# Moving half of the q/k projections of a batch into that batch, in an attention and feed-forward kernel on one core

## The chip, the cores and the metric

The kernel runs on one core of a Trainium2 chip. The metric is device time in microseconds. Times are given to 0.01 us; three runs of the kernel before lie between 1335.29 and 1335.87 us.

## What is computed

The input x has 4 batches of 1024 tokens with 256 features, in float32. One attention block with 16 heads of 16 features is followed by a gated feed-forward block; both have a layer norm before and after, and a residual:

```python
def attn(x, Wqkv, Wout):                      # B, S, D = 4, 1024, 256; H, Dh = 16, 16
    q, k, v = split((x @ Wqkv.T))             # each (B, H, S, Dh)
    scores = einsum("bhqd,bhkd->bhqk", q, k) / sqrt(Dh)
    e = exp(clip(scores - max(scores), -50, 50))
    a = e / (sum(e) + 1e-6)
    return concat_heads(a @ v) @ Wout.T

x = x + layernorm(attn(layernorm(x), Wqkv, Wout))
h = silu(x1 @ w1.T * s1) * (x1 @ w2.T * s2)   # x1 = layernorm(x); 256 -> 1024
h = gelu(h @ h1.T * s3); h = gelu(h @ h2.T * s4)   # 1024 -> 1024, twice
x = x + layernorm(h @ w3.T * s5)              # 1024 -> 256
```

## The kernel before

**Attention, 0 to about 658 us.** It runs batch by batch (b, four), then by group of four heads (g, four), then by half of the 512 queries (h, two). One (b, g, h) is a *unit*: 16 score tiles of 128 keys by two heads by 512 queries. For a tile TensorE makes scores (`s`, L451), ScalarE takes the exponential (`e`, L452, with no maximum subtracted), and TensorE adds `e` times the values into `acc` (L459). The score tiles have three buffers (`ps`), the exponentials a ring of eight tiles. VectorE keeps a running maximum of the exponentials (`top`, L468, in `rise`), which enters the denominator.

**The main loop (L868).** One pass, called a *turn* here, makes three score tiles, adds one or two pairs of finished tiles into `acc`, and then calls `side.take()` (L563). There are 32 units and about five and a third turns to a unit, some 170 turns in all. The work around the scores is a set of chains of `Step`s. A turn goes through the chains in order, first those in `first`, then those in `rest`, and takes from each what its `gap` allows (the number of turns since the chain's last step). **At most one step that uses TensorE is run in a turn**; steps that do not use TensorE are not limited. The PSUM tile of these steps, `misc`, has one buffer, so that a step's result must have been copied out by VectorE before the next step's matmul starts.

**What is in the chains.** `prologue(b)` makes the steps of a batch's input: layer norm statistics (`gather`, `root`), normalisation (`apply`), transposition (`transposes`, `xT`), and the projections. `project(w, m, h)` (L320) makes q (w = 0) or k (w = 1) for eight heads (m = 0 or 1, that is groups 0 and 1, or groups 2 and 3) and 512 tokens: two 128x512 matmuls (four passes in the profile, `p` L324), then two copies on VectorE: `hi` (L269) and `lo`, the rest beside `hi` (L328). `values(t)` makes v (`pv`, L315). `cq` holds q and k of one batch, with one buffer for each (w, m, hi or lo); `stack(b, g)` copies them with 32 DMAs on SP's queue into `stacks` (L413), which the scores read. It is called at the end of a unit, two groups ahead (L609 to L616), together with `slots`, a copy of v on GpSimd (L429).

**The bound.** Since no maximum is subtracted, `total` (sums of k, L349 and L350), `squares` (ScalarE, L338), `bound` (L357: four small bf16 matmuls `pn` in one `misc` tile, and a maximum on VectorE), `gauge` and `flag` (`pr`) work out per batch whether the scores can be too large. `flags` is the list of these steps.

**The end of a unit.** `unit_end` (L594) copies `acc` out (`o`, L269) and puts `divide` into the chains (`po`, L478 and L480, eight transposes in a score buffer: `side.borrowed` makes the next turn start with one tile fewer). After a batch's last group `ending` follows: transposes of the result (called `po` too, L506), the output projection `py` (L516), a layer norm and the residual, in the first turns of the next batch.

**Order of a batch's input before.** `begin(b)` (L583) puts one chain for batch b + 1: statistics, normalisation, transposes and the four projections of m = 0. When group 1 of batch b ends (g == NG - 3), v and, five turns later, the four projections of m = 1 (`qk1`) are added, and after them `flags`. So all of a batch's q and k are made during the preceding batch. Beside these run the rounding of the feed-forward weights (`check_weights`, with DMAs on GpSimd's queue, and two VectorE instructions `w` L257 for each block).

**Feed-forward, from about 658 us.** Dense matmuls (L697) that read weights from the places that q and k had; the change does not edit it.

Of the kernel before, what the change touches and what calls it, by code (L numbers as in the profile page):

```python
# [9 lines left out]
F32 = mybir.dt.float32  # L10
F32R = mybir.dt.float32r
BF16 = mybir.dt.bfloat16
I32 = mybir.dt.int32
AF = mybir.ActivationFunctionType
ALU = mybir.AluOpType
AX = mybir.AxisListType
PSUM = bass.MemoryType.PSUM

P = 128
HEADS = 16  # L20
DH = 16
SLOT = 32
HPG = P // SLOT
NG = HEADS // HPG
# [13 lines left out]
TPQ = NQ // P  # L38
# [76 lines left out]
def tile_fast(ctx: ExitStack, tc: tile.TileContext, x, wqk, wv, wo, w1, w1s, w2, w2s, h1, h1s, h2, h2s, w3, w3s, out, bad):  # L115
    nc = tc.nc
    B, S, D = x.shape
    HID = w1.shape[1]
    DC = D // P
    HC = HID // P  # L120
    NT = S // P
    NH = S // NQ
    HPT = P // DH
    GPT = HPT // HPG
# [52 lines left out]
    with ExitStack() as actx, ExitStack() as rctx:  # L177
# [90 lines left out]
        def to_vector(o, i, scale=1.0):  # L268
            nc.vector.tensor_scalar(o, i, scale, None, ALU.mult)  # L269

        def prologue(b, space, copy):

            st = {}
# [46 lines left out]
            def project(w, m, h):  # L320
                def run():
                    pp = space(f"p{w}_{b}_{m}_{h}")
                    for c in range(DC):
                        nc.tensor.matmul(pp, wqk_sb[:, c, w, HPT * m : HPT * (m + 1), :], st["xT"][:, c, h * NQ : (h + 1) * NQ], start=c == 0, stop=c == DC - 1)  # L324
                    hi, lo = (cq[w, m, k][:, h * NQ : (h + 1) * NQ] for k in ("hi", "lo"))
                    scale = 1.0 if w else 1.0 / math.sqrt(DH)
                    copy(hi, pp, scale)
                    nc.vector.scalar_tensor_tensor(lo, pp, scale, hi.bitcast(F32), ALU.mult, ALU.subtract)  # L328

                return run  # L330

            kinds = [(w, m) for w in range(2) for m in range(DC)]

            def squares(w, m, h):
                def run():
                    sq = st["sq", w, m] = work.tile([P, NQ], BF16, tag="sq", name="sq", bufs=4)
                    hi = cq[w, m, "hi"][:, h * NQ : (h + 1) * NQ].bitcast(F32)
                    nc.scalar.activation(sq, hi, AF.Square)  # L338

                return run  # L340

            def total(m):
                def run():
                    if m == 0:
                        st["norm"] = work.tile([P, NT], F32, tag="norm", name=f"norm_{b}", bufs=1)
                        st["sum"] = work.tile([P, DC], F32, tag="sum", name="sum", bufs=1)
                        st["sum2"] = work.tile([P, DC], BF16, tag="sum2", name="sum2", bufs=1)
                    t = st["sum"][:, m : m + 1]
                    nc.vector.tensor_reduce(t, cq[1, m, "hi"].bitcast(F32), AX.X, ALU.add)  # L349
                    nc.gpsimd.tensor_tensor(st["sum2"][:, m : m + 1], t, t, ALU.mult)  # L350

                return run

            def bound(h):


                def run():  # L357
                    pn = space(f"pn_{b}_{h}")
                    for k, (w, m) in enumerate(kinds):
                        nc.tensor.matmul(pn[SLOT * k : SLOT * (k + 1), :], heads_bf, st["sq", w, m], start=True, stop=True)  # L360
                    nc.vector.tensor_reduce(st["norm"][:, TPQ * h : TPQ * (h + 1)], pn.rearrange("p (t n) -> p t n", n=P), AX.X, ALU.max)

                return run

# [7 lines left out]
            def flag():  # L372

                pr = space(f"pr_{b}")
                for i in range(2):
                    nc.tensor.matmul(pr[0:1, i * P : (i + 1) * P], st["kinds"][:, i : i + 1], ident, start=True, stop=True)
                for m in range(DC):
                    nc.tensor.matmul(pr[0:1, 2 * P + SLOT * m : 2 * P + SLOT * (m + 1)], st["sum2"][:, m : m + 1], heads_bf, start=True, stop=True)

                qs, ks = (pr[0:1, 0 : 2 * P].rearrange("p (i w n) -> p i w n", i=2, w=2)[:, :, w, :] for w in range(2))  # L380
                top = work.tile([1, P // 2], F32, tag="ktop", name="ktop", bufs=1)
                nc.vector.tensor_reduce(top, ks.rearrange("p i n -> p n i"), AX.X, ALU.max)

                nc.vector.scalar_tensor_tensor(top, top, S * S / SPREAD, pr[0:1, 2 * P : 2 * P + P // 2], ALU.mult, ALU.add)
                bounds = work.tile([1, 2, P // 2], F32, tag="bounds", name="bounds", bufs=1)
                nc.vector.tensor_mul(bounds, qs, top.unsqueeze(1).to_broadcast([1, 2, P // 2]))
                most = work.tile([1, 2], F32, tag="most", name="most", bufs=1)
                nc.vector.tensor_reduce(most, bounds, AX.X, ALU.max)
                k = counts + 2 * b

                for i, limit in enumerate((SAFE, math.log(S / FULL))):
                    limit = 0.98 * limit * limit * S * S / (1 + SPREAD)
                    nc.vector.tensor_scalar(misses[0:1, k + i : k + i + 1], most[:, i : i + 1], limit, 0.0, ALU.is_le, ALU.is_equal)
# [2 lines left out]
            xt = [[Step(apply(h, i), 1, False) for i in range(0, TPQ, 2)] + [Step(transposes(h, c), 1) for c in range(DC)] for h in range(NH)]  # L396
            qk = [[[Step(project(w, m, h), 1) for w in (1, 0)] for h in range(NH)] for m in range(DC)]
            v = [Step(values(t), 1) for t in range(0, NT, 2)]
            flags = [Step(total(m), 1, False) for m in range(DC)]
            for h in range(NH):  # L400
                flags += [Step(squares(w, m, h), 1, False) for w, m in kinds] + [Step(bound(h), 1)]
            return norm, xt, qk, v, flags + [Step(gauge, 0, False), Step(flag, 1)]

        def copies(g, w, c0=0, c1=S):

# [19 lines left out]
        def slots(b, g, t0=0, t1=NT):  # L425


            def run():
                nc.gpsimd.tensor_copy(  # L429
                    vaug[g % 2][:, t0:t1, :, 0:DH], cv[:, t0:t1, HPG * DH * g : HPG * DH * (g + 1)].rearrange("p t (h e) -> p t h e", e=DH)  # L430
                )
                slotted[g % 2] = b, g, t1

            return run
# [116 lines left out]
        class Side:  # L551
# [4 lines left out]
                self.borrowed = False  # L556

            def add(self, steps, first=False):
                chain = [list(steps), self.slot]
                (self.first if first else self.rest).append(chain)  # L560
                return chain

            def take(self):  # L563
# [16 lines left out]
        side = Side()  # L580
        accs, tops, ends, later = {}, {}, {}, {}

        def begin(b):  # L583

            if b + 1 < B:
                norm, xt, qk, v, flags = prologue(b + 1, misc, to_vector)

                qk1 = sum(qk[1], [])
                qk1[0].gap = 3
                later["rest"] = v, qk1 + [Step(lambda: side.add(flags), 0, False)]  # L590

                later["chain"] = side.add([Step(lambda: None, 0 if b else 4, False)] + sum((norm[h] + xt[h] for h in range(NH)), []) + sum(qk[0], []))

        def unit_end(b, g, h):  # L594

            o = both.tile([P, NQ], F32, tag="o", name="o", bufs=2)
            to_vector(o, accs[b, g, h])

            assert g or not b or not any(step.tensor for step in ends[b - 1, h][0])
            unit = side.add(divide(g, h, o, tops[b, g, h]), True)  # L600
            if g == NG - 1:
                unit[0].extend(ending(b, h, to_scalar if (b, h) == (B - 1, NH - 1) else to_vector))
                ends[b, h] = unit
            if h < NH - 1:
                return

            n, at = g + 2, b
            if n >= NG:
                n, at = n - NG, b + 1  # L609
            if b == B - 1 and g == NG - 2:  # L610
                load_weights("h1", range(HC // 2))
            if at < B:
                if at > b:
                    assert not later["chain"][0]
                stack(at, n)
                slots(at, n)()  # L616
            if g == NG - 3 and b + 1 < B:
                v, qk1 = later["rest"]
                assert not later["chain"][0]
                later["chain"][0].extend(v)  # L620
                side.add([Step(lambda: None, 5, False)] + qk1)
            elif g == NG - 3:
                side.add([Step(lambda n=n: load_weights(n), 1, False) for n in ("w1", "w2", "w3")])
                side.add([Step(lambda: None, 7, False)] + prepare(0, to_vector))
            if g == NG - 1:
                begin(b + 1)


# [196 lines left out]
        def first_copy(*args):  # L825
            (to_scalar if alone else to_vector)(*args)

        norm, xt, qk, v, flags = prologue(0, first_space, first_copy)

        queues = [nc.scalar] + [nc.gpsimd, nc.sync] * 3 + [nc.gpsimd]  # L830

# [20 lines left out]
        stack(0, 1)  # L852
        load_rest()
        early = [v[1], Step(slots(0, 0, 0, NT // 2), 0, False)]
        side.add(early + v[2:] + [Step(slots(0, 0), 0, False), Step(slots(0, 1), 0, False)] + sum(qk[1], []) + [Step(lambda: side.add(flags), 0, False)])
        begin(0)
        side.add([s for k in blocks for s in check_weights(*k)])
        made = seen = weighed = 0

# [270 lines left out]
```

## Time and profile before

| | us |
|---|---|
| median of three runs | 1335.56 (1335.29 to 1335.87) |
| the profiled execution, its own time | 1335.65 |
| its span in the profile | 1333.7 |
| busy in the span: PE, PEld, DVE, ACT, POOL | 1271.8, 797.1, 724.3, 696.6, 120.7 |
| from the first unit's end to the last unit's end | 57.63 to 658.44 |
| batch 1, 2, 3 from unit end to unit end | 161.43, 157.59, 140.58 |

PE is TensorE's matmuls, PEld its weight loads, DVE VectorE, ACT ScalarE, POOL GpSimd. The span is what the trace covers; the execution's own time is 1.95 us longer. A line such as L324 is a line of the kernel before. In a row of the timeline the first number is the start, the second the length.

### The profile page before, as it was taken

How to read it: one execution, taken by the hardware profiler on the slowest of the kernel's cores; microseconds unless marked ns; L12 is line 12 of the kernel's file. 1: busy time of each engine (PE TensorE's matmuls, PEld its weight loads, DVE VectorE, ACT ScalarE, POOL GpSimd, SP SyncE). 2: the span in 40 equal slices, each digit the busy share in tenths (PEclk: the TensorE clock that was granted, in tenths of full speed). 3: DMA queues.
4: the chain of work that ended last, by engine and by line, in shares of the span. 5: the costliest groups of instructions: out<-in, count | busy, mean ns of one | idle time of the engine just before them, and what ended most of it. 6: DMA issues, size and time to landing. Idle time of an engine off the chain costs nothing.

```text
span 1333.7 us, 18779 instructions
## 1 busy us (share of the span) xinstructions
PE 1271.8 (95%) x7042; PEld 797.1 (60%) x7042; DVE 724.3 (54%) x1561; ACT 696.6 (52%) x847; POOL 120.7 (9%) x166
## 2 busy tenths in 40 slices
PE   7999999999999999989999999999999999999996
PEld 3334333343343434333478888888888888888885
DVE  3575669756696455645482553735436364362623
ACT  4587788877887787888741321414224141231410
POOL 6120112111111000000000000000000000000000
PEclk9999999999999999999999999999999999999998
DMA  4675344544444433235220000000000000000000
GB/s 133 152 194 111 98 97 113 122 111 99 120 106 106 77 64 62 45 64 179 79 111 1 1 16 1 17 0 0 16 1 16 0 16 2 0 17 0 17 0 19
DMA packets 38661, 79.61 MB, mean 60 GB/s; under 512 B 11296, under 2 KB 21152, under 8 KB 38560
## 3 DMA queue, kind: packets, MB, share of 16 engines
q1 hardware_dynamic: 30672, 53.66, 18.3%
q0 software_dynamic: 7360, 24.12, 5.5%
q8 instruction: 58, 0.95, 0.3%
q10 hardware_dynamic: 528, 0.52, 0.1%
q14 instruction: 43, 0.35, 0.1%
HBM read 28.98 MB, written 15.73 MB: 34 GB/s over the span
## 4 chain that ended last, share of the span: by engine, by line
PE 78%; DVE 9%; ACT 7%; issue 2%; POOL 1%; DMA 0%; SPq 0%; ACTq 0%; POOLq 0%; DVEq 0%
PE ph L697 35%; PE acc L459 13%; PE s L451 8%; ACT e L452 6%; PE pg L697 6%; PE pz L750 4%; PE p L324 4%; PE py L516 2%; PE pv L315 2%; DVE top L468 2%; PE po L480 1%; DVE o L269 1%; DVE sg L713 1%; DVE st L93 1%; DVE ha_lo L702 1%
## 5 line engine op out<-in xcount | busy, mean ns | idle before, releaser
L452 ACT ACTIVATE e<-s 128x1024 f32<-128x1024 f32 x512 | 486.3, 1036 | 131.1 <-PE s L451 117.8
L459 PE MATMUL acc<-e,vaug 128*32 128x512 f32 x2048 | 256.5, 603 | 2.9 <-POOL vaug L429 2.9
L733 ACT ACTIVATE a<-ph,h_scale 128x512 f32<-128x512 f32 x128 | 81.0, 685 | 306.9 <-PE ph L697 306.9
L451 PE MATMUL s<-sq,sk 64*128 64x512 f32 x1024 | 193.9, 449 | 24.7 <-ACT e L452 22.7
L697 PE MATMUL ph<-hb_lo,h 128*128 128x512 f32 x512 | 199.4, 389 | 0.0
L697 PE MATMUL ph<-hb_hi,h 128*128 128x512 f32 x512 | 199.4, 389 | 0.0
L451 PEld LDWEIGHTS s<-sq,sk 64*128 64x128 f32 x1024 | 86.3, 184 | 159.4 <-ACT e L452 124.5
L468 DVE TENSOR_TENSOR top<-top,e 128x512 f32<-128x512 f32 x192 | 134.1, 699 | 35.7 <-ACT e L452 30.1
L459 PEld LDWEIGHTS acc<-e,vaug 128*32 128x32 f32 x2048 | 49.4, 109 | 108.5 <-issue 98.1
L734 DVE CAST ha_hi<-a 128x512 fp32r<-128x512 f32 x64 | 27.1, 424 | 158.2 <-ACT a L733 158.2
L103 POOL TENSOR_TENSOR rstd<-ve,minus_half 128x4 f32<-128x4 f32 (+1 forms) x33 | 37.5, 1136 | 791.6 <-DVE ve L101 791.6
L697 PEld LDWEIGHTS ph<-hb_lo,h 128*128 128x128 f32 x512 | 96.1, 188 | 20.1
L697 PEld LDWEIGHTS ph<-hb_hi,h 128*128 128x128 f32 x512 | 96.1, 188 | 20.2
L697 PE MATMUL ph<-ha_hi,sq 128*128 128x512 f32 x256 | 101.9, 398 | 0.4
L697 PE MATMUL ph<-ha_lo,sq 128*128 128x512 f32 x256 | 99.8, 390 | 0.0
L697 PE MATMUL ph<-ha_lo,sk 128*128 128x512 f32 x256 | 99.7, 390 | 0.0
L697 PE MATMUL ph<-ha_hi,sk 128*128 128x512 f32 x256 | 99.7, 390 | 0.0
L713 DVE SCALAR_TENSOR_TENSOR sg<-pg,w_scale,sg 128x512 f32<-128x512 f32 x64 | 47.1, 745 | 47.7 <-ACT sg L711 47.7
L711 ACT ACTIVATE sg<-pg,w_scale 128x512 f32<-128x512 f32 x64 | 43.3, 688 | 56.6 <-DVE ha_lo L702 48.4
L734 DVE CAST hb_hi<-a 128x512 fp32r<-128x512 f32 x64 | 27.0, 422 | 82.2 <-ACT a L733 82.2
L324 PE MATMUL p<-xT,wqk_sb 128*128 128x512 f32 x128 | 64.0, 626 | 0.9 <-ACT xT L266 0.9
L697 PEld LDWEIGHTS ph<-ha_hi,sq 128*128 128x128 f32 x256 | 48.2, 188 | 12.7 <-DVE sg L713 3.4
(145 smaller groups left out, 1663.6 us busy)
## 6 DMA issues: line engine op xcount, KB each, us to landing
w<-in_h_dram POOLq DMA_DIRECT2D x16, 512.0 KB, 4.6
h_r<-wr POOLq DMA_DIRECT2D x16, 512.0 KB, 3.8
sk<-ck1hi SPq DMA_DIRECT2D x64, 64.0 KB, 2.3
sk<-ck1lo SPq DMA_DIRECT2D x64, 64.0 KB, 2.3
sq<-cq1hi SPq DMA_DIRECT2D x64, 64.0 KB, 2.3
sq<-cq1lo SPq DMA_DIRECT2D x64, 64.0 KB, 2.3
h<-h_r SPq DMA_DIRECT2D x8, 512.0 KB, 6.5
sk<-ck0hi SPq DMA_DIRECT2D x56, 64.0 KB, 2.3
```

The source lines that it names most:

```text
L103: nc.gpsimd.tensor_tensor(rstd[:, :n], ve[:, :n], self.minus_half[:, :n], ALU.pow)
L324: nc.tensor.matmul(pp, wqk_sb[:, c, w, HPT * m : HPT * (m + 1), :], st["xT"][:, c, h * NQ : (h + 1) * NQ], start=c == 0, stop=c == DC - 1)
L451: nc.tensor.matmul(s[:, a, :], stacks[1, g % 2, u][r, c * P : (c + 1) * P], stacks[0, g % 2, u][r, h * NQ : (h + 1) * NQ], start=True, sto ...
L452: nc.scalar.activation(pair(k)[:, u], s, AF.Exp)
L459: nc.tensor.matmul(acc[SLOT * i : SLOT * (i + 1), :], vaug[g % 2][:, c, i, :], pair(k)[:, i // 2, i % 2, :], start=c == 0, stop=c == NT - 1)
L468: nc.vector.tensor_max(top, top if c > 1 else pair(k - 2)[:, :, :, 0:P], pair(k)[:, :, :, 0:P])
L697: nc.tensor.matmul(p, homes[n][c][:, m * P : (m + 1) * P], half[:, c, :], start=c == 0 and k == 0, stop=c == len(homes[n]) - 1 and k == 1)
L711: nc.scalar.activation(sg, p[:, 0, :], AF.Silu, scale=scales["w1"][:, m : m + 1])
L713: nc.vector.scalar_tensor_tensor(sg, p[:, 1, :], scales["w2"][:, m : m + 1], sg, ALU.mult, ALU.mult)
L733: nc.scalar.activation(a, p[:, j, :], AF.Gelu, scale=scales[n][:, m : m + 1])
L734: nc.vector.tensor_copy(o[0][:, m, :], a)
L750: nc.tensor.matmul(p[t], half[:, c, t * P : (t + 1) * P], homes["w3"][c], start=c == 0 and k == 0, stop=c == HC - 1 and k == 1)
```

## The change

It has four parts.

1. The projections of m = 1 (q and k of heads 8 to 15) are no longer made in the preceding batch. `begin(b)` puts those of batch b itself at the head of all chains (`first=None`, a new case of `Side.add`), with a gap of two turns from batch 1 on. For batch 0, where they had been early already, v and these projections form that leading chain.
2. `begin(b)` starts only the statistics of batch b + 1, both halves together. Its transposes, projections of m = 0 and the bound of m = 0 are added by `go_on`, when the leading chain is through.
3. v is a chain of its own, begun at the same place as before (the end of group 1). `slots` of the next batch is put behind v if v is not through.
4. The bound is split by m: `bound(m, h)` uses two of the four small matmuls and a maximum over 64 partitions; there are four for a batch instead of two. `norm`, `sum` and `sum2` have two buffers. The layout of the flag's reductions follows (its last product is made in two instructions).

The diff, cut to its core:

```diff
@@ prologue
-            def bound(h):
+            def bound(m, h):
                 def run():
-                    pn = space(f"pn_{b}_{h}")
-                    for k, (w, m) in enumerate(kinds):
-                        nc.tensor.matmul(pn[SLOT * k : SLOT * (k + 1), :], heads_bf, st["sq", w, m], start=True, stop=True)
-                    nc.vector.tensor_reduce(st["norm"][:, TPQ * h : TPQ * (h + 1)], pn.rearrange("p (t n) -> p t n", n=P), AX.X, ALU.max)
+                    pn = space(f"pn_{b}_{m}_{h}")
+                    for w in range(2):
+                        nc.tensor.matmul(pn[SLOT * (2 * m + w) : SLOT * (2 * m + w + 1), :], heads_bf, st["sq", w, m], start=True, stop=True)
+                    own = slice(2 * SLOT * m, 2 * SLOT * (m + 1))
+                    nc.vector.tensor_reduce(st["norm"][own, TPQ * h : TPQ * (h + 1)], pn[own, :].rearrange("p (t n) -> p t n", n=P), AX.X, ALU.max)
...
-            flags = [Step(total(m), 1, False) for m in range(DC)]
-            for h in range(NH):
-                flags += [Step(squares(w, m, h), 1, False) for w, m in kinds] + [Step(bound(h), 1)]
-            return norm, xt, qk, v, flags + [Step(gauge, 0, False), Step(flag, 1)]
+            flags = []
+            for m in range(DC):
+                flags.append([Step(total(m), 1, False)])
+                for h in range(NH):
+                    flags[m] += [Step(squares(w, m, h), 1, False) for w in range(2)] + [Step(bound(m, h), 1)]
+            flags[-1] += [Step(gauge, 0, False), Step(flag, 1)]
+            return norm, xt, qk, v, flags
@@ begin
-        def begin(b):
-
-            if b + 1 < B:
-                norm, xt, qk, v, flags = prologue(b + 1, misc, to_vector)
-
-                qk1 = sum(qk[1], [])
-                qk1[0].gap = 3
-                later["rest"] = v, qk1 + [Step(lambda: side.add(flags), 0, False)]
-
-                later["chain"] = side.add([Step(lambda: None, 0 if b else 4, False)] + sum((norm[h] + xt[h] for h in range(NH)), []) + sum(qk[0], []))
+        def begin(b, lead=()):
+
+            _, _, qk, _, flags = own.pop(b)
+            if b + 1 < B:
+                own[b + 1] = prologue(b + 1, misc, to_vector)
+                norm, xt, qk_next, v, flags_next = own[b + 1]
+
+                later["chain"] = side.add([Step(lambda: None, 0 if b else 4, False)] + sum(norm, []))
+                later["v"] = v
+
+            def go_on():
+                side.add(flags[0] + flags[1] if b == 0 else flags[1])
+                if b + 1 < B:
+
+                    later["chain"][0].extend(sum(xt, []) + sum(qk_next[0], []) + flags_next[0])
+
+            left = sum(qk[1], [])
+            for step in left:
+                step.gap = 2 if b else 1
+            later["left"] = side.add(list(lead) + left + [Step(go_on, 0, False)], None)
@@ unit_end
                 stack(at, n)
-                slots(at, n)()
+                if at > b and later["v"]:
+                    assert n == 0
+                    later["v"].append(Step(slots(at, n), 0, False))
+                else:
+                    slots(at, n)()
             if g == NG - 3 and b + 1 < B:
-                v, qk1 = later["rest"]
-                assert not later["chain"][0]
-                later["chain"][0].extend(v)
-                side.add([Step(lambda: None, 5, False)] + qk1)
+                v = later["v"]
+                later["v"] = side.add(v)[0]
...
-            if g == NG - 1:
+            if g == NG - 1 and b + 1 < B:
                 begin(b + 1)
```

## The prediction

> **What bounds the kernel now.** I read the page's busy times first, then the same by stage (the windows view cut at the `o` copies that end each batch), then the TensorE timeline in a crowded and in an empty stretch, last VectorE's timeline at a batch's start.
>
> ```profile
> PE 1271.8 (95%) x7042; PEld 797.1 (60%) x7042; DVE 724.3 (54%) x1561; ACT 696.6 (52%) x847; POOL 120.7 (9%) x166
> L452 ACT ACTIVATE e<-s 128x1024 f32<-128x1024 f32 x512 | 486.3, 1036 | 131.1 <-PE s L451 117.8
> ```
>
> PE at 95% hides two regimes, which the stages show (columns: stretch, its length, busy PE, PEld, DVE, ACT, POOL, clock, DMA):
>
> ```profile
> 57.63:198.84 141.21, 135.00 (x849) 53.50 (x850) 89.59 (x181) 109.49 (x122) 22.73 (x32) 0.99 0.52 127
> 198.84:360.27 161.43, 152.74 (x981) 61.61 (x981) 111.24 (x245) 126.34 (x138) 29.59 (x37) 1.00 0.46 110
> 360.27:517.86 157.59, 149.93 (x967) 60.91 (x968) 102.24 (x219) 123.68 (x136) 18.80 (x24) 1.00 0.40 86
> 517.86:658.44 140.58, 128.38 (x889) 48.24 (x889) 78.28 (x168) 121.28 (x131) 5.25 (x6) 1.00 0.37 85
> ```
>
> The last batch, which prepares no other, is 17 to 21 us shorter than batches 1 and 2, and TensorE idles 12.2 us in it. So the side work costs time where it stands. A turn with a projection, from batch 1 (three score tiles, one or two pairs into `acc`, the projection):
>
> ```profile
> 260.93 0.96 PE L451 MATMUL s<-sq,sk 64*128 64x512 f32 x6
> 261.82 1.06 PE L459 MATMUL acc<-e,vaug 128*32 128x512 f32 x8
> 262.82 1.98 PE L324 MATMUL p<-xT,wqk_sb 128*128 128x512 f32 x4
> 264.73 0.97 PE L451 MATMUL s<-sq,sk 64*128 64x512 f32 x6
> 265.63 1.92 PE L459 MATMUL acc<-e,vaug 128*32 128x512 f32 x16
> 267.49 1.98 PE L324 MATMUL p<-xT,wqk_sb 128*128 128x512 f32 x4
> ```
>
> Nothing stands in brackets: TensorE never waits. The first turn takes 264.73 - 260.93 = 3.80 us, the second to 269.40, 4.67 us. Two turns with no side step, in batch 3:
>
> ```profile
> 599.71 0.96 PE L451 MATMUL s<-sq,sk 64*128 64x512 f32 x6
> 600.61 1.06 PE L459 MATMUL acc<-e,vaug 128*32 128x512 f32 x8
> 601.60 0.51 PE L451 MATMUL s<-sq,sk 64*128 64x512 f32 x2
> 602.30 0.49 PE L451 MATMUL s<-sq,sk 64*128 64x512 f32 x2 [0.20 <-ACT e L452]
> 603.22 0.50 PE L451 MATMUL s<-sq,sk 64*128 64x512 f32 x2 [0.42 <-ACT e L452]
> 603.64 1.92 PE L459 MATMUL acc<-e,vaug 128*32 128x512 f32 x16
> 605.50 0.96 PE L451 MATMUL s<-sq,sk 64*128 64x512 f32 x6
> ```
>
> They take 1.89 and 3.90 us, and TensorE waits for exponentials between. At a batch's start a third resource is full: after 198.84 no row of VectorE's timeline up to 213.90 has an idle time before it, for example
>
> ```profile
> 206.29 0.66 DVE L468 TENSOR_TENSOR top<-top,e 128x512 f32<-128x512 f32 x1
> 206.87 0.73 DVE L111 TENSOR_SCALAR y<-y,mv,rstd 128x256 f32<-128x256 f32 x2
> 207.52 0.68 DVE L269 TENSOR_SCALAR oT<-po 128x512 f32<-128x512 f32 x1
> ```
>
> [...] PE is over 90% busy in all four batches, with and without waits. [...] four `pn` take 0.40 us together, one 384 ns; so two will cost nearly what four do. [...]
>
> **The change part by part.** In both programs' instruction order TensorE has the same scores, `acc`, projections, v and transposes; only `pn` comes in 16 groups of two instead of 8 of four. I counted the turns by their side step: 51 with a dear one (`p`, `pv`, `py`) in both, 31 with a divide and 28 with a light one (`pt`, `po` L506, `fpt`) in both, with `pn` or `pr` 12 before and 20 after, empty 43 before and 35 after.
>
> *Projections.* Units between `o` copies: 415.96 to 437.33 has four projections, 21.37 us; the three from 573.25 to 623.95 have none and are 16.90 on average. So one costs (21.37 - 16.90) / 4 = 1.12 us (1.91 of TensorE, less waits that it fills). Batch 0 loses four (-4.5), batch 3 gains four (+4.5), batches 1 and 2 lose and gain four: 0. The new place in batch 3 decides. It isn't among its empty turns: the projections alternate with `po` L506 and `py` in the batch's first seven turns, and the divide of unit 0 waits behind them. These turns are TensorE's already, so I take the full price. Its bounds: 1.5 at most (a projection in a turn with two `acc` pairs against the 3.1 us of three exponentials), 0.3 at least (two turns, one with a projection and one without, are 6.5 us of TensorE against 6.2 of three-tile exponentials twice). No DMA moves: the 32 DMAs on SP stay at the unit's end, some four turns after the last projection, where they had been ready far longer; cost 0, and a few us of their lateness are covered by a whole group before the copies are read. GpSimd's four more products lie beside everything; its v copies keep their unit ends, since v ends a turn before.
>
> *The bound.* Eight empty turns become `pn` turns: a turn with `pn` or `pr` takes 3.00 us on average, an empty one 2.78, so 8 x 0.22 = +1.8 us. Bounds: 0 and 3.5 (their eight maxima, 8 x 0.69 = 5.5 us of VectorE, two thirds exposed, as VectorE is about two thirds busy).
>
> *Less crowding.* Dear turns straight after a dear one fall from 34 to 25. Means of turns by own and preceding kind, times the new counts, give +1.0 in place of +1.8: -0.8.
>
> *Squares.* ScalarE's squares outside turns with a dear step fall from 25 to 17. Six turns of one shape took 20.51 us with four squares (319.04 to 339.55) and 19.79 without (605.50 to 625.29): 0.18 each, so -1.4; bounds 0 and 8 x 0.6 = -4.8.
>
> *VectorE at the batch's start.* In batch 1's first unit (198.84 to 218.12, 19.28 us) VectorE idles 0.77 us: 18.5 us of work. After come two projections' copies (4 x 0.62 from start to start), four more statistics with their ends (4 x 0.55) and a root (0.17); two `y` copies (1.24) and four normalisations (1.3) leave: +2.3, 20.8 us, 1.5 more than the unit. The copies of a projection free the only `misc` tile, so what is late on VectorE delays the next side step of TensorE, with scores and `acc` queued behind it. Batch 2 (360.27 to 379.74, idle 0.72): 18.7 + 2.3 = 21.0 against 19.47, 1.5 too. In batch 3 VectorE has no such load, 0. Of these 3.0 us I take two thirds, +2.0, as the next unit has less to do; bounds 0 (all dissolves there) and 4 (the copies also wait for their projections, with the rest queued behind them).
>
> *Divides.* The delayed divide of unit 0 comes to stand in the turn before unit 1's in batch 2, two turns before in batches 1 and 3. Each takes one of three score buffers, and leaves ScalarE short: a divide turn is 3.37 us after a dear turn, about 4.5 after an empty one. I take 1.2 for the neighbours and 0.3 for each of the others, +1.8; bounds 0 and 3.
>
> Sum: 0 + 1.8 - 0.8 - 1.4 + 2.0 + 1.8 = +3.4 us. The profiled execution took 1335.65 us (span 1333.7 and 1.95 around it), 0.09 above the median; 1335.65 + 3.4 = 1339.05, 1339.0 beside the median.
>
> **The rivals.** A measurement of this kernel can tell about 0.2%, 2.7 us, from no change: below 1332.9 is faster, above 1338.2 slower.
> - *Spreading pays* (faster). Batch 3's 12.2 us of idle TensorE take up its four projections at 0.3 each: +1.2 - 4.5 + 1.8 - 0.8 - 1.4 = -3.7, 1332.0. It decides once a projection there costs under half its price in batch 0. For it: the waits in the empty turns. Against it: the new places are beside `py`, where no wait stands.
> - *Zero sum* (same). VectorE's lag dissolves and the divides don't collide: 0 + 1.8 - 0.8 = +1.0, 1336.6. For it: equal counts of dear turns.
> - *VectorE becomes the bound* at the starts of batches 1 and 2 (slower by more): 4 for its lag, 3 for the divides, 1.8 for `pn`: +8.8, 1344.4. For it: the timeline without gaps; against it: after one unit the load falls to 13 us a unit.
> - That the projections don't move isn't open: the order shows them in the batch's first turns.
>
> **How the numbers follow.** My sum 0.46, spreading 0.16, zero sum 0.22, VectorE 0.16. The sum's own spread puts some 0.38 of its 0.46 above 1338.2 and the rest within. Slower 0.38 + 0.16 = 0.54; faster 0.15; same 0.31. Range: 1332.5 (just above spreading's full gain) to 1344.5 (VectorE's case).
>
> **What would show it.** Batch 0 from unit end to unit end about 4 to 5 us shorter than its 141.21, batch 3 about 5 us longer than its 140.58, batches 1 and 2 longer by 1 to 3 us each; after a batch's start TensorE's side steps wait for VectorE, and `s` waits for `e` around the paired divides; feed-forward unchanged at 675 us. Wrong would be batch 3 growing by under 2 us, or batches 1 and 2 shrinking.

## The result and the profile after

The changed kernel takes **1338.55 us** (median of 11 runs, 1337.74 to 1341.84). The kernel before, run beside it, takes 1335.56 us (median of 11 runs, 1334.27 to 1338.57). The ratio is 1.0022, with a 95% interval of 1.0013 to 1.0031: slower by 3.0 us. The prediction was 1339.0 us, 1332.5 to 1344.5, slower at 0.54.

The profiled execution of the changed kernel took 1339.87 us (span 1338.1), 4.2 us more than the profiled one before, so the trace holds about one microsecond more than the medians do. Of the code lines shown here, those from 324 on have moved down by 2 to 6: `p` is now L326, the divide's transposes `po` L484 and L486, the running maximum `top` L474.

The page's busy times of the changed kernel, and its costliest group:

```profile
PE 1274.8 (95%) x7042; PEld 798.9 (60%) x7042; DVE 731.7 (55%) x1573; ACT 697.9 (52%) x847; POOL 118.8 (9%) x166
L458 ACT ACTIVATE e<-s 128x1024 f32<-128x1024 f32 x512 | 486.5, 1033 | 134.4 <-PE s L457 119.5
```

As many matmuls as before; TensorE is busy 3.0 us longer, VectorE 7.4 us. The averages say no more than that. The same four stages as before, cut at the `o` copies that end each batch (stretch, its length, busy PE, PEld, DVE, ACT, POOL, clock, DMA):

```profile
57.70:190.21 132.51, 125.64 (x833) 50.34 (x834) 86.71 (x178) 109.45 (x122) 21.41 (x31) 1.00 0.56 135
190.21:354.54 164.33, 153.39 (x977) 62.21 (x977) 112.78 (x247) 126.67 (x138) 28.21 (x37) 0.99 0.46 108
354.54:516.10 161.56, 151.90 (x971) 61.88 (x972) 104.53 (x223) 124.40 (x136) 18.60 (x24) 0.99 0.38 83
516.10:662.88 146.78, 136.14 (x901) 50.92 (x901) 84.78 (x179) 121.41 (x131) 6.17 (x7) 0.99 0.37 82
```

Batch 0 is 8.7 us shorter than its 141.21, batches 1, 2 and 3 are 2.9, 4.0 and 6.2 us longer. After 662.88 come 675.2 us of feed-forward, against 675.3 before. So 13.1 us are lost in three batches and 8.7 us are won in the first; 4.4 us are left between these two executions, and 3.0 us between the medians.

**Batch 3** has the four projections in its first seven turns. TensorE's timeline of the changed kernel there, then in a later turn of the batch, without a side step:

```profile
524.78 0.96 PE L457 MATMUL s<-sq,sk 64*128 64x512 f32 x6
525.67 1.06 PE L465 MATMUL acc<-e,vaug 128*32 128x512 f32 x8
527.60 1.98 PE L326 MATMUL p<-xT,wqk_sb 128*128 128x512 f32 x4 [0.86 <-DVE oT L269]
529.51 0.73 PE L457 MATMUL s<-sq,sk 64*128 64x512 f32 x4
...
585.52 0.50 PE L457 MATMUL s<-sq,sk 64*128 64x512 f32 x2 [0.34 <-ACT e L458]
586.44 0.50 PE L457 MATMUL s<-sq,sk 64*128 64x512 f32 x2 [0.41 <-ACT e L458]
587.35 0.50 PE L457 MATMUL s<-sq,sk 64*128 64x512 f32 x2 [0.41 <-ACT e L458]
587.79 3.22 PE L465 MATMUL acc<-e,vaug 128*32 128x512 f32 x16
```

In the first, the bracket says that the projection stood 0.86 us until VectorE had copied the `oT` that precedes it out of `misc`; that turn takes 529.51 - 524.78 = 4.73 us and not 3.80. In the second, 16 matmuls take 3.22 us and not 1.92: TensorE's granted clock was halved from 588.3 us on, for 3.41 us. That turn takes 5.41 us, and 4.12 in the kernel before. Such a stretch does not come in every execution: in the traces of experiments 1, 2 and 6, which have the four projections and no halved clock in batch 3, the batch takes 145.2 us, 4.6 more than before and not 6.2.

**Batch 0** holds, beside the 4.5 us of the forecast, a gain that nothing in the prediction foresaw. TensorE's timeline at the first divide, before:

```profile
57.86 0.63 PE L478 MATMUL po<-ident,top 128*128 128x128 f32 x4 [2.20 <-DVE top L468]
58.37 0.66 PE L480 MATMUL po<-ident,o 128*128 128x128 f32 x4
58.95 0.94 PE L451 MATMUL s<-sq,sk 64*128 64x512 f32 x4
59.83 3.33 PE L459 MATMUL acc<-e,vaug 128*32 128x512 f32 x16
```

and after, where a projection (55.66) stands ahead of the divide:

```profile
58.46 1.92 PE L465 MATMUL acc<-e,vaug 128*32 128x512 f32 x16
60.32 0.66 PE L484 MATMUL po<-ident,top 128*128 128x128 f32 x4
60.81 0.60 PE L486 MATMUL po<-ident,o 128*128 128x128 f32 x4
```

Before, the divide waited 2.20 us for VectorE's running maximum, and then 16 matmuls took 3.33 us in place of 1.92: TensorE's clock was halved, from 59.3 us for 3.41 us. After, neither. The two turns took 5.26 + 6.48 us before and 3.80 + 3.77 us after, 4.2 us less for the same steps.

**Batches 1 and 2** give up and take on four projections each, and are together 6.9 us longer. The worst turn is that of the divide of batch 2's unit 1. TensorE's timeline there, before:

```profile
394.76 1.92 PE L459 MATMUL acc<-e,vaug 128*32 128x512 f32 x16
396.62 0.66 PE L478 MATMUL po<-ident,top 128*128 128x128 f32 x4
```

after:

```profile
394.49 1.92 PE L465 MATMUL acc<-e,vaug 128*32 128x512 f32 x16
396.34 0.50 PE L457 MATMUL s<-sq,sk 64*128 64x512 f32 x2
399.51 0.66 PE L484 MATMUL po<-ident,top 128*128 128x128 f32 x4 [2.67 <-DVE top L474]
400.11 0.75 PE L486 MATMUL po<-ident,o 128*128 128x128 f32 x4
400.79 1.22 PE L457 MATMUL s<-sq,sk 64*128 64x512 f32 x4
401.94 1.93 PE L465 MATMUL acc<-e,vaug 128*32 128x512 f32 x8
```

and VectorE's after, over the same time:

```profile
396.40 0.42 DVE L494 TENSOR_TENSOR on<-po,den 128x256 f32<-128x256 f32 x1
396.75 0.68 DVE L257 SCALAR_TENSOR_TENSOR w<-w,wr 128x512 f32<-128x512 f32 x1
397.35 0.08 DVE L257 DVE_READ_ACCUMULATOR w<-w,wr 128x1 f32 x1
397.35 2.10 DVE L474 TENSOR_TENSOR top<-top,e 128x512 f32<-128x512 f32 x2
399.38 0.68 DVE L269 TENSOR_SCALAR o<-acc 128x512 f32<-128x512 f32 x1
```

The divide's first transposes need the unit's last running maximum. VectorE has no idle time here: the maximum stands behind the previous divide's arithmetic, a layer norm and a weights' block, and is done only at 399.45. TensorE works in order, so scores and `acc` wait behind the transposes for 2.67 us; then eight matmuls take 1.93 us instead of 1.06, the clock halved again, from 400.5 us for 3.41 us. The turn took 7.50 us against 4.79 before with the same steps; the next, with a transposition step more, 4.08 against 2.02 (1.68, if its last score tile is counted with the turn after it).

How much of this is the halved clock, the kernel of experiment 8 shows. Up to batch 3 it has the same steps as the changed kernel and the same waits, but no halved clock in batches 1 and 2:

```profile
400.16 0.66 PE L484 MATMUL po<-ident,top 128*128 128x128 f32 x4 [2.67 <-DVE top L474]
400.76 0.65 PE L486 MATMUL po<-ident,o 128*128 128x128 f32 x4
401.35 0.73 PE L457 MATMUL s<-sq,sk 64*128 64x512 f32 x4
402.01 1.06 PE L465 MATMUL acc<-e,vaug 128*32 128x512 f32 x8
```

The wait is again 2.67 us, but the eight matmuls take 1.06. Its batches 1 and 2 take 162.90 and 160.20 us, 1.5 and 2.6 more than in the kernel before. So of the 6.9 us, 4.1 come from the steps and their waits, and 2.8 from the two halved stretches.

### The profile page after: what moved, and what is told of

Its sections match the earlier page's. It is cut to its first block, busy times and chain, and to the rows that moved or that the text cites. A ratio compares the mean times of both kernels' runs of the same rounds, so it can differ in the third digit from the quotient of the medians.

```text
span 1338.1 us, 18787 instructions
## 1 busy us (share of the span) xinstructions
PE 1274.8 (95%) x7042; PEld 798.9 (60%) x7042; DVE 731.7 (55%) x1573; ACT 697.9 (52%) x847; POOL 118.8 (9%) x166
## 4 chain that ended last, share of the span: by engine, by line
PE 75%; DVE 12%; ACT 7%; issue 3%; SPq 1%; DMA 1%; ACTq 0%; POOL 0%; POOLq 0%; DVEq 0%
PE ph L721 35%; PE acc L465 13%; PE s L457 8%; ACT e L458 6%; PE pz L774 4%; PE pg L721 4%; PE p L326 4%; PE py L522 2%; DVE top L474 2%; PE pv L317 2%; DVE sg L737 1%; PE po L486 1%; DVE st L93 1%; DVE o L269 1%; DVE ha_lo L726 1%
## 5 line engine op out<-in xcount | busy, mean ns | idle before, releaser
L474 DVE TENSOR_TENSOR top<-top,e 128x512 f32<-128x512 f32 x192 | 136.2, 710 | 34.8 <-ACT e L458 29.0
L326 PE MATMUL p<-xT,wqk_sb 128*128 128x512 f32 x128 | 63.9, 625 | 4.2 <-DVE oT L269 3.1
```

Of the source, the lines that this page charges most:

```text
L474: nc.vector.tensor_max(top, top if c > 1 else pair(k - 2)[:, :, :, 0:P], pair(k)[:, :, :, 0:P])
```

## The experiments

"Turn 95" is the turn of 7.50 us, counted from 0 (the very first pass, which has nothing to add into `acc` yet, is left out); batches 1, 2 and 3 begin at turns 43, 86 and 128. Each kernel was timed beside the kernel before, whose medians were 1335.57, 1335.70 and 1337.16 us in the three sittings; ratios are to the runs beside, and not always the quotient of two such medians. What is said against the changed kernel by medians is against its 1338.55 us, from yet another sitting. "At one clock" compares runs whose mean granted TensorE clock was the same; the table after experiment 9 has them.

**1. The bound of m = 0 left out of batches 1 to 3.**

```diff
+                        nc.vector.memset(st["norm"], 0.0)
-                    ... + [Step(bound(m, h), 1)]
+                    ... + ([Step(bound(m, h), 1)] if m or not b else [])
```

> The changed kernel without the bound's matmuls and maxima for m = 0 in batches 1 to 3: six turns with two pn become empty turns (the squares and sums stay; norm is set to 0, so this part of the bound is left out). The prediction's price of a pn turn is 0.22 us: 6 x 0.22 = 1.3 us less than the changed kernel's 1338.55, about 1337.2. Rival one: pn lies beside waits anyway, 0 to 0.5 us less. Rival two: pn also makes TensorE wait for the squares on ScalarE and holds the one misc tile until VectorE is done, 3 us less or more.

Measured: 1339.89 us (1337.96 to 1341.56), ratio 1.0026 (1.0014 to 1.0037). By medians not faster than the changed kernel, at one clock 0.3 us faster (five runs against two), where 1.3 was forecast. The trace shows `pv` steps moving into the turns that lost their `pn`. So the added `pn` turns cost little, if anything, and the loss is elsewhere.

**2. and 3. The delayed divide put at the head of the chains**, in batch 2 alone (the first line added) and in every batch (the second), so that it follows its unit at once and no two divides are neighbours:

```diff
-            unit = side.add(divide(g, h, o, tops[b, g, h]), True)
+            unit = side.add(divide(g, h, o, tops[b, g, h]), None if (b, g, h) == (2, 0, 0) else True)
+            unit = side.add(divide(g, h, o, tops[b, g, h]), None if (g, h) == (0, 0) else True)
```

> The changed kernel, with the divide of batch 2's first unit put at the head of all chains, so that it comes right after its unit and not in the turn before the next unit's divide. Theory of the paired divides: turns 95 and 96 of the changed kernel took 7.50 and 4.08 us against 4.79 and 1.68 before, and at the same place now there is one divide alone: 3 to 5 us less than 1338.55, about 1334.5. Rival (VectorE's lag): the divide only meets VectorE's backlog there, and wherever it is moved the backlog is paid: at most 1 us less. Rival (price as predicted): 1.2 us less, 1337.3.

> The same for the first unit of every batch; in batches 1 and 3 the two divides stood two turns apart. Theory of the paired divides: batches 1 and 3 give about 0.5 to 1 us each beyond the run with batch 2 alone, 1333 to 1334. Rival (prediction's price): 1.8 us less than 1338.55 in all, 1336.8. Rival (VectorE's lag): at most 1 us less in all.

Measured: 1342.05 us (1339.46 to 1345.78), ratio 1.0049 (1.0033 to 1.0066), and 1346.93 us (1345.58 to 1348.85), ratio 1.0087 (1.0070 to 1.0104): 3.5 and 8.4 us slower than the changed kernel, at one clock 2.5 and 6.6. No expectation had them slower. TensorE's timeline of the first of them at the divide that was moved:

```profile
372.58 1.06 PE L465 MATMUL acc<-e,vaug 128*32 128x512 f32 x8
377.38 1.09 PE L484 MATMUL po<-ident,top 128*128 128x128 f32 x4 [3.74 <-DVE top L474]
378.26 1.06 PE L486 MATMUL po<-ident,o 128*128 128x128 f32 x4
379.25 1.22 PE L457 MATMUL s<-sq,sk 64*128 64x512 f32 x4
380.40 3.32 PE L465 MATMUL acc<-e,vaug 128*32 128x512 f32 x16
```

Straight after its unit the divide waits 3.74 us, with no second divide near it, and turn 95 is still 6.63 us long with its neighbour gone. The theory of paired divides falls: a divide waits for the running maximum wherever it comes soon after its unit while VectorE is behind.

**4. The next batch's statistics behind the four projections** (batches 1 and 2):

```diff
-                later["chain"] = side.add([...] + sum(norm, []))
+                later["chain"] = side.add([...] + ([] if b else sum(norm, [])))
-                    later["chain"][0].extend(sum(xt, []) + ...)
+                    later["chain"][0].extend((sum(norm, []) if b else []) + sum(xt, []) + ...)
```

> The changed kernel, with the statistics of the next batch's input (in batches 1 and 2) taken only when the batch's own four projections are through, so that VectorE has about 5 us less to do in the crowded turns. Theory of VectorE's lag: turns 45, 46, 48, 88, 90 and 91 of the changed kernel are 0.7 to 1.2 us each above what TensorE alone needs in them, about 5 us; the prediction counted 2.0. So 2 to 4 us less than 1338.55, 1334.5 to 1336.5. Rival: the lag is made up by the copies that wait for their projections, not by the statistics, and the paired divides stay: within 0.7 us of 1338.55.

Measured: 1340.29 us (1338.88 to 1341.84), ratio 1.0035 (1.0023 to 1.0048), 1.7 us slower than the changed kernel by medians, and no different at one clock (one run against two). The batch's first turns do get shorter (turns 45, 46 and 48 by 0.6, 0.8 and 0.8 us). But the statistics now stand ahead of the maximum that the next divides need. VectorE's and TensorE's timelines of this kernel in batch 1:

```profile
234.66 0.42 DVE L93 BATCH_NORM_STATS2 st<-x 128x6 f32<-128x256 f32 x1
...
235.86 1.00 DVE L101 TENSOR_SCALAR ve<-mv 128x4 f32<-128x4 f32 x1
236.77 0.68 DVE L474 TENSOR_TENSOR top<-top,e 128x512 f32<-128x512 f32 x1
```

```profile
237.59 1.08 PE L484 MATMUL po<-ident,top 128*128 128x128 f32 x4 [4.00 <-DVE top L474]
```

The divide in turn 53 waits 4.00 us, and the turn takes 8.53 us instead of 4.30; turn 95 takes 9.55. Batches 1 and 2 come out at 164.59 and 161.48 us, against 164.33 and 161.56. Moved within VectorE's queue, the work took the loss with it.

**5. A later divide.** After units of group 0 the divide comes two turns later than otherwise (a gap of three in place of one):

```diff
-            return [Step(run, 1)]
+            return [Step(run, 3 if g == 0 else 1)]
```

> The changed kernel, with the divides of group 0 (both halves, all batches) run two turns after their unit's end at the earliest. New theory (the divide waits for VectorE): a divide's first transposes need the unit's last running maximum, which stands behind VectorE's backlog in the first two units of a batch; the run with the divide right after the unit (7.55 and 7.57 us for that turn) lost 2.5 us more at each place. Two turns later the maximum should be there: turn 95's 7.50 falls to about 3.4 to 4.3 and the halved TensorE clock that followed goes, turn 53 gains about 1: 3 to 6 us under the changed kernel's 1338.55, 1333 to 1335.5. Rival (the backlog is a fixed amount of VectorE work, paid by the next side step wherever the divide stands): within 1 us of 1338.55. Rival (paired divides, score buffers): the divides are still three turns apart, 2 to 4 us less, without a change of the wait for the maximum.

Measured: 1337.84 us (1335.4 to 1342.18, 22 runs), ratio 1.0016 (1.0008 to 1.0023), 0.7 us less than the changed kernel (0.7 to 1.2 at one clock), about as the rival of the fixed backlog had it. Turn 95 falls from 7.50 to 4.06 us; turns 96 and 99 give back 1.7 and 2.4. The side steps that now come first need VectorE as well.

**6. Less work for VectorE: the rounding of the weights pauses in the first 14 turns of batches 1 to 3.** Nothing is left out; its two VectorE instructions for each block, its casts on GpSimd and its DMAs, come later.

```diff
                 for chain in self.first + self.rest:
+                    if chain is later.get("weights") and self.slot < later.get("hold", 0):
+                        continue
...
         def begin(b, lead=()):
+            later["hold"] = side.slot + 14 if b else 0
...
-        side.add([s for k in blocks for s in check_weights(*k)])
+        later["weights"] = side.add([s for k in blocks for s in check_weights(*k)])
```

> The changed kernel, with the chain that rounds the feed-forward weights paused in the first 14 turns of batches 1 to 3; about four VectorE instructions of 0.7 us in each of the first two units go elsewhere, to places with empty turns. Theory (the divide and the side steps wait for VectorE's backlog): 2.4 us less VectorE work in batch 1's and in batch 2's first two units, so 2 to 4 us under 1338.55, 1334.5 to 1336.5, with shorter turns 45 to 48, 88 to 91 and 95. Rival (the backlog is made by copies that wait for their projections): within 0.7 us of 1338.55.

Measured: **1334.22 us** (1330.97 to 1335.24, 22 runs), ratio 0.9981 (0.9975 to 0.9988): 4.3 us less than the changed kernel. TensorE's timeline at turn 95:

```profile
397.28 0.66 PE L484 MATMUL po<-ident,top 128*128 128x128 f32 x4 [1.05 <-DVE top L474]
```

1.05 us in place of 2.67, no halved clock behind it, and 5.80 us for the turn. Turns 45 and 46 fall from 5.82 and 3.28 to 5.23 and 2.64, turns 90 and 96 from 5.02 and 4.08 to 4.42 and 2.70. This is the experiment that carries the theory: with the change's own steps all in place, pausing other work of VectorE takes the loss away. At turn 95 the wait is 1.62 us shorter. VectorE's timelines there show 1.2 us of it as two weights' blocks (0.61 us each, from start to start) that are gone from ahead of the maximum, and 0.4 as the unit's last two maxima, which take 1.70 us in place of 2.10 beside GpSimd's copy `vaug`. The pause also takes work off GpSimd and its DMA queue, and no run takes it off VectorE alone.

**7. The same pause in the kernel before.**

> The kernel before, with the same hold as in e5_hold (the rounding of the feed-forward weights pauses in the first 14 turns of batches 1 to 3); nothing else is changed. In the changed kernel the hold brought 1338.55 to 1334.22, 4.3 us. Theory (the crowd on VectorE at the starts of batches 1 and 2 is the change's doing: its copies of projections came on top of the statistics and the weights' rounding): the kernel before has no such crowd, so the hold brings it little, 0 to 1.5 us, 1334.2 to 1335.7, about where the changed kernel with the hold stands; the divides of units 0 and 1 in batch 2 keep their turns of about 5 us. Rival (the weights' rounding costs that much at any batch's start, with the change or without it): 4 us here too, 1331.5, and the changed kernel stays 3 us behind the kernel before whatever is held.

Measured: 1335.64 us (1334.58 to 1337.88, 14 runs), ratio 0.9998 (0.9990 to 1.0006): no gain against 1335.70, and 1.5 us against the median of its own sitting, 1337.16. At one clock the pause brings the kernel before 2.1 to 2.3 us (0.6 at 0.994, a single run), and the changed kernel 3.9 to 4.2. In the traces, without the 1.6 us of one halved stretch in each kernel with the pause, batches 1 and 2 get 1.7 us shorter in the kernel before and 4.6 in the changed one (against the trace of experiment 8). So about half of what the pause removes, or more, is a crowd that the change made; theory and rival were both right in part. The rival's other half fails: with the pause in both, the changed kernel is not 3 us behind but 0.7 to 0.8 us ahead at 0.992 and 0.993.

**8. and 9. The price of the four projections in each place.** In the changed kernel those of batch 3 are left out, in the kernel before those that batch 0 makes for batch 1:

```diff
-            left = sum(qk[1], [])
+            left = sum(qk[1], []) if b < B - 1 else []
```

```diff
-                qk1 = sum(qk[1], [])
+                qk1 = sum(qk[1], []) if b else [Step(lambda: None, 0, False)]
```

> The changed kernel without the four m = 1 projections of batch 3 (left out, the scores there read the q and k of batch 2): their price in the new place. The prediction: 4.5 us (4 x 1.12), so 1334.0; the trace's batch 3 grew by 6.2 us, of which a halved clock window is about 1.3, so up to 5: 1333.5. Rival (spreading pays): 1.2 us, 1337.3.

> The kernel before without the four m = 1 projections that batch 0 makes for batch 1 (left out, the scores of batch 1 read batch 0's q and k): their price in the old place. The prediction: 4.5 us, 1331.1. Rival (batch 0's 8.6 us shorter trace after the change is all projections): 8 us, 1327.5. If it is about 4.5, the other 4 us of batch 0's gain come from the first unit's divide, which waited 1.9 us longer before and was followed by a halved clock.

Measured: 1332.38 us (1329.37 to 1335.06, 18 runs), ratio 0.9971 (0.9963 to 0.9979), and 1332.66 us (1329.85 to 1335.49, 22 runs), ratio 0.9975 (0.9967 to 0.9984). In the new place the four cost 1338.55 - 1332.38 = 6.2 us, in the old one 1335.70 - 1332.66 = 3.0. Both prices need a correction, since TensorE's clock differed between the runs. The mean spans (us) of the runs with three of the mean granted clocks, the number of runs in brackets:

| kernel | 0.992 | 0.993 | 0.994 |
|---|---|---|---|
| before | 1336.0 (21) | 1335.3 (26) | 1333.4 (41) |
| changed | 1337.1 (2) | 1336.4 (5) | none |
| 1: no bound of m = 0 | 1336.8 (5) | none | none |
| 2: divide first, batch 2 | 1339.6 (2) | none | 1337.7 (1) |
| 3: divide first | 1343.7 (1) | none | none |
| 4: statistics later | 1337.1 (1) | none | none |
| 5: later divide | 1336.4 (9) | 1335.2 (2) | 1335.1 (7) |
| 6: pause | 1332.9 (4) | 1332.5 (3) | 1330.6 (8) |
| 7: pause, before | 1333.7 (2) | 1333.2 (5) | 1332.8 (1) |
| 8: none in batch 3 | 1331.2 (2) | 1330.8 (12) | none |
| 9: before, none in batch 0 | none | 1330.6 (7) | 1329.6 (2) |
| 10: pause and later divide | none | none | 1329.5 (2) |

At one clock the new place costs 5.6 to 5.9 us and the old one 3.8 to 4.7; the turns that held them in the old place (29 to 37) shrink by 4.2 in the trace. Without the four, batch 3 takes 139.60 us, 5.6 less than with them and no halved clock, but also 1.0 less than in the kernel before: there the other side steps fall on other turns. So the move from batch 0 to batch 3 is dearer by up to 3 us, and its exact size stays open. The table also splits the result: at one clock the changed kernel is 1.1 us behind, and the rest of its 3.0 us goes with a median clock of 0.992 against 0.994. The clock need not be a cause from outside, though. In the changed kernel's profiled execution three halved stretches lie inside the attention after its start, from 284.5, 400.5 and 588.3 us, where the kernel before has one, at 59.3.

**10. Pause and later divide together**, in the changed kernel:

> The changed kernel with both the hold of e5_hold and the late divide of e9_late_divide (after units of group 0 a divide comes three turns after its unit and not one). Theory (a divide only shows VectorE's backlog, and the hold has removed most of the backlog): turn 95 falls from e5_hold's 5.80 to about 4, a neighbour gives part of it back, and the time is that of e5_hold within 1 us, 1333.5 to 1335. Rival (the divide's wait and the backlog are two costs that add): 4.3 + 0.7 us and the 1.8 of turn 95, 1332.0 to 1333.

Measured: **1330.28 us** (1329.16 to 1333.83, 6 runs), ratio 0.9961 (0.9946 to 0.9976). It beats both kernels, and is 8.3 us below the changed one, where the two edits alone gave 4.3 and 0.7. Both expectations were too high, the theory's by more. At a clock of 0.994 both together are at 1329.5 us of span (2 runs) and the pause alone at 1330.6 (8 runs): there the later divide brings 1.1 us, about what it brings without the pause, and the two edits about add, as the rival said. The rest of the 8.3 us goes with the clock. TensorE's waits for the running maximum and for the flag's `kinds` from 195 to 480 us (us in total, times, longest), for the kernel before, the changed one, the pause and both:

```profile
PE po L478 <- DVE top L468: 1.9, 5, 0.8
```

```profile
PE po L484 <- DVE top L474: 4.3, 4, 2.7
PE pr L378 <- DVE kinds L372: 2.1, 1, 2.1
```

```profile
PE po L484 <- DVE top L474: 2.6, 4, 1.1
PE pr L378 <- DVE kinds L372: 2.1, 1, 2.1
```

```profile
PE po L484 <- DVE top L474: 0.6, 2, 0.3
```

In batch 1 both together are 3.2 us shorter in the trace than the pause alone (159.26 against 162.49): in the new order of steps the flag's `pr` no longer waits 2.1 us, and no halved clock follows. In batch 2 they are 1.6 us longer (159.16 against 157.60): turn 95 falls from 5.80 to 4.07, but turns 96 and 99 take 0.9 and 1.7 us more. So even with the backlog removed a part is handed to the next side steps, as in experiment 5. The wait of `pr` is followed by a halved clock at 284.5 us in the changed kernel and at 286.3 us in the kernel with the pause. With both edits the profiled execution has no halved clock between 15.3 and 1319.2 us, and three of the six runs had a mean clock of 0.996, where 106 runs of the kernel before reach 0.995 at most. Its batch 3 is 4.2 us longer than that of the kernel before, close to the predicted price of four projections, and batches 1 and 2 together 0.6 us shorter.

## Why the prediction was right, and where only by cancelling

The time, the sign and the feed-forward were right, and so was the outline: batch 0 shorter, batch 3 longer, a loss at the starts of batches 1 and 2. That +3.4 came so near to the measured 3.0 us is luck in part, since only 1.1 of the 3.0 are left at one clock, and the sum had no term for the clock. Step by step:

- **Projections, 4.5 us in each place.** Right for the old place (3.0 by medians, 3.8 to 4.7 at one clock, 4.2 in the trace). For the new place the two readings differ: leaving the four out saves 5.6 to 6.2 us, 1.4 to 1.55 us each and not 1.12, but batch 3 grew by only 4.6 us where no halved clock lies in it. The other 1.6 of its 6.2 us are that clock. "In batch 3 VectorE has no such load, 0" was wrong: the timeline shows a projection there waiting 0.86 us for VectorE's copy of `oT`, in every trace with these projections, so that this wait is within the 4.6.
- **The bound, +1.8.** Its parts came as forecast (two `pn` take 0.39 us where four took 0.40; the maximum over 64 partitions takes 677 to 695 ns, that over 128 took 657 to 692); the price in time is not shown. Experiment 1 took six of the eight added groups away and gained nothing by medians, and 0.3 us at one clock. The averages of turns "with `pn`" and "empty" came from turns that differ in more than the `pn`; an added step moves the others.
- **Less crowding -0.8, squares -1.4.** Not tried by themselves; open.
- **VectorE at the batch's start, +2.0, and the divides, +1.8.** The mechanism of the first was right. Together they were to cost 3.8, 0.3 of it in batch 3. Batches 1 and 2 grew by 4.1 where their clock was not halved (the trace of experiment 8), which is near, and by 6.9 with two halved stretches; the pause takes all of the 4.1 away. The reason given for the second was wrong. Score buffers and ScalarE do not make the divide dear; it waits for the running maximum behind VectorE's backlog (2.67 us in turn 95), and pairing adds little: in experiment 2, without its neighbour, turn 95 still takes 6.63 of the 7.50 us (the neighbour's arithmetic is itself a part of the backlog). So `s` does not wait for `e` around the divides, as was expected: there, ScalarE waits for `s` (3.26 us in turn 95). The prediction counted what VectorE had to do and divided it by the unit's length; it did not ask which of VectorE's instructions TensorE stands in front of.
- **Batch 0, -4.5.** It became 8.7 shorter. The missing 4.2 us are the first divide's wait of 2.20 us and the halved clock, both in the trace of before at 57.9 to 63 us. That turn was not looked at, since the batch as a whole seemed to lose only projections.

The sum was to be -4.5 in batch 0 and about +8 in the others; it was -8.7 and +13.1 in the trace. Without the three halved stretches the +13.1 would be 8.7 (1.5, 2.6 and 4.6), close to the forecast. So two things that the prediction did not price had opposite signs and nearly cancelled: 4.2 us won at the first divide of batch 0, and 4.4 us lost to halved clocks later. Of the rivals, "VectorE becomes the bound" named the place of the loss in batches 1 and 2, with a size (1344.4) that is too high. The 1336.6 of "zero sum" lies below the interval of the ratio (1337.3 to 1339.7 us), but its +1.0 is what is left at one clock; its reasons fail, since VectorE's lag did not dissolve. "Spreading pays" had put 1.2 us for the four projections in batch 3, and is refuted by the 4.6 of the traces and the 5.6 to 6.2 of experiment 8.

## What to carry to other kernels

When steps are moved to another time, look there for the in-order wait with the most behind it: here TensorE's transposes in front of one VectorE result, with scores and accumulation queued after them (2.67 us in turn 95). VectorE was late here, and moving a step mostly moved the loss (experiments 2 to 4: 1.7 to 8.4 us slower than the changed kernel by medians, experiment 5: 0.7 faster). What helped was to take work off that engine for the time of the crowd, and then to give the waiting step more distance (experiments 6 and 10: 4.3 and 8.3 us faster). Compare runs at one mean clock as well as by medians, and turns one by one and not by the mean of their kind, since a right total can hide two errors.

## What the runs showed of the hardware

**The halved clock.** In the traces of the two kernels each stretch of halved clock lasts 3.41 us, but for the last, which runs to the end of the trace (from 1325.7 us before, from 1329.0 after). In the changed kernel's trace the starts at 11.4, 284.5, 400.5 and 588.3 us lie 273.1, 116.1 and 187.7 us apart, 80, 34 and 55 times the 3.413 us of one stretch. TensorE is 95% busy over the span, and its waits ahead of these stretches are 2.10 us ahead of 284.5 and 2.67 ahead of 400.5 (2.20 ahead of 59.3 in the kernel before); ahead of 588.3 there are only three of 0.34 to 0.41, between score matmuls, and the kernel before has the same three (at 582.7 to 584.5) without a halved clock. That the waits cause it is argued from their place, not shown by a run of its own.

The same wait is not followed by a halved clock each time. In the trace of experiment 8 TensorE waits 2.67 us at the same step as in the changed kernel, and the eight matmuls after it take 1.06 us and not 1.93. What decides is not shown. The spread of the changed kernel's runs fits: 1336.4 us of span at a mean clock of 0.993 (five runs), 1340.0 at 0.989 (one).

**VectorE beside GpSimd.** In the changed kernel the last `top` before the divide in turn 95 took 1.31 us, and the one before it 0.69; GpSimd's copy `vaug` ran from 398.27 to 398.90, and the maximum ended 0.55 us later. It had started first, at 398.14, and was longer by 0.62 us, the whole length of the copy. In experiment 4 a `ve` of four elements took 1.00 us, where one 1.3 us earlier took 0.17, and ended within 0.02 us of GpSimd's cast of weights. That GpSimd's work lengthened the two is argued from the overlap, not shown by a run of its own. In both places TensorE was waiting for a maximum in the same queue (2.67 and 4.00 us), so if it did so, work on an engine that is 9% busy lengthened the path by some 0.6 and 0.8 us, an estimate from these four times.
